# A message-passing layer on one Trainium2 core: v's products among the tiles of the sums, a head in halves, and a reordered end

## The chip, the cores and the metric

The program runs on one core of a Trainium2 chip. The metric is the device time of one execution in microseconds (us), as a median of several executions. Engines are called by their short names: PE does the matrix products (PEld is its loading of weights), DVE and ACT do elementwise work, POOL issues the indirect DMAs here, and SP issues the other DMAs.

## The reference

A graph has N = 12500 nodes with 128 features, and 412500 edges with 20 features and a weight each. The edges come sorted by `dst`; their `src` is in no order.

```python
h = jnp.maximum(_layernorm(x, axis=-1), 0.0)
# inside the layer: idx_i = src, idx_j = dst, f_ij = edge_attr_20, rcut_ij = edge_weight
def ssp(x):
    return jax.nn.softplus(x) - LOG2
h = x @ W_in2f                                   # x is the h above
Wij = ssp(f_ij @ W_f1 + b_f1) @ W_f2 + b_f2
Wij = Wij * rcut_ij[:, None]
x_ij = h[idx_j] * Wij
agg = jax.ops.segment_sum(x_ij, idx_i, num_segments=h.shape[0])
out = ssp(agg @ W_o1 + b_o1) @ W_o2 + b_o2
...
    x = x + _L0_gnn_ref(h, ...)
    return x
```

So each edge gets a filter vector (two small layers with a softplus between), which is multiplied with the row of h of its dst; the products, called messages here, are summed by src, and a two-layer output is added to x.

## The kernel before, in words

**Tiles and stages.** The edges are worked through in 806 chunks of 512, four chunks to a group. A chunk has QT = 4 tiles of 128 edges. `step(k)` (L993) is called once for each chunk k, and for a while after the last one; it holds one link of a software pipeline, so that it touches chunks k to k+6 and more. The instruction order on every engine is the order in which the code issues them (a manual schedule, the loop at L1216). A queue runs its instructions in that order, and an instruction that waits holds up all behind it on its engine.

The way of a chunk c through the pipeline:

- *hidden* (PE, L691): the edge features times W_f1, for a pair of chunks at once, into the PSUM tile z of 2 x 512 columns.
- *log* (ACT, L700, L701, L703): absolute value, exponential and logarithm, which make the softplus, again 2 x 512 wide. `softplus_logs` (L403 to L405) is the exponential and the logarithm alone; the finish uses it 512 wide behind its own absolute value (L439).
- *end* (DVE, L709): max(z, -b) plus that logarithm gives r.
- *bias* (ACT, L793): a PSUM bank of tag "v" is filled with a bias row; *value* (PE, L801) adds r @ W_f2 to it in four products. This is v, the filter of the chunk.
- *window* (DVE, L785) and *pick* (PE, L812): a one-hot matrix picks the rows of h of the dst nodes out of a window of rows ("near") that SP loads; *picked* (ACT, L822) multiplies them with the edge weight and gives hg.
- *blocks*, *rank* (DVE L714, PE L733 and L766, DVE L738): for each edge, the place of its message in a table of slots.
- *message* (DVE, L830): o = v * hg, and POOL issues four indirect DMAs (L834) that scatter the 512 rows to their slots.

The tag "v" has three PSUM banks, which v and the picked rows share.

**Segments and sums.** The 202 groups are cut in 7 segments of 88, 44, 30, 14, 14, 8 and 4 groups. Each segment has its own table of slots, with room for each block of 128 nodes. Seven steps (DELAY) after the last chunk of a segment, its table is read back while later chunks go on: a Collect loads units of up to 6 tiles (SP, L873), *compare* (DVE, L886) makes one-hot matrices `to`, *add* (PE, L907) sums tile after tile into a PSUM bank that holds four blocks of nodes ("acc"), and *keep* moves a finished bank to `agg` (ACT, L928, for the first segment; an add on DVE, L930, for the others). Which units are summed in which step is planned ahead (L1070 to L1102): a rate in tiles a step follows from the work left and from `end = NCH + BEYOND`, and at most one bank ends in a step. The units of a step are compared in it; the adds come one unit later, so that one unit is always left over.

So there are steps without sums (before the first segment is done) and steps with sums, some steps with sums alone after the last chunk, and then a last part in which the last segment is summed and the output layers (*finish*, L428) run, quad by quad of 512 nodes.

**The order in a step.** In step k the code issues: the loads; the message of k and its scatters; what is left of the ranks (DVE); keep for the banks that the step before finished (DVE or ACT); picked(k+1) on ACT and value(k+1) on PE; pick(k+2) on PE and bias(k+2) on ACT; window (DVE); end (DVE); blocks (DVE); the compares (DVE); rank (PE); log (ACT); hidden (PE); the adds of the sums (PE). On PE alone this is value, pick, rank, hidden, sums, and then the next step's value. A first product of value, pick and hidden also waits for a scatter of eight chunks earlier (BACK = 8, `behind`).

**Head.** Before the loop the first quads of h are made: `make_h` (L326 to L393) normalises 512 rows of x, multiplies them with W_in2f and splits the result (PSUM, hps) in three bf16 parts: hb's first is a copy (L367), the rest goes to a tile `left` in SBUF (DVE, L370), its bf16 copy is the second (L371), and the rest of that the third (DVE, L373). The bias of the features' layer and its product with W_f2 are made in `biases` (L302, its matmul L307, DVE's L308). The parts are stored, and the window's rows are loaded from there. The loop starts at k = -3.

**x for the end.** The output is added to x. From step XK = 300 on quads of x are loaded ahead (`x_ahead`, NX = 14 of 25 quads early), and the bias b_o2 is added to them (`x_bias`, on DVE for the early ones, on POOL for those after the last chunk) from a row spread over all partitions in SBUF (bo2).

## Time and profile before

| | us |
|---|---|
| median of ten executions | 5290.81 |
| the ten, lowest to highest | 5267.05 to 5316.33 |
| the profiled execution, its own time | 5285.38 |
| its span | 5283.6 |

| engine | busy us | share of the span | instructions |
|---|---|---|---|
| PE | 3706.6 | 70% | 21594 |
| PEld | 2833.7 | 54% | |
| DVE | 3140.5 | 59% | 7101 |
| ACT | 2788.9 | 53% | 5466 |
| POOL | 3145.4 | 60% | 3292 |

The clock that PE was granted was 0.764 of full speed on the mean. The DMA engines moved 820.65 MB, 155 GB/s.

A busy time is the time in which an engine had an instruction in work; what an engine spends on issuing a DMA or on waiting is not in it. In the rows of the trace, a mark such as [0.49 <-DVE to L886] says that the engine had been idle for 0.49 us before the instruction and what released it; x22 counts the instructions that the row puts together; `out<-in` gives the tiles that an instruction writes and reads. A PE product shows as two records (f32). A stretch is given from the span's start in us. The profiled execution is one of the program as it runs, so a sum of durations from it is made against its own time, and not against the median.

### The profile page before, as it was taken

What the parts mean: (1) busy time and instruction counts of PE and PEld (TensorE: products, weight loads), DVE (VectorE), ACT (ScalarE), POOL (GpSimd) and SP (SyncE); (2) the same over time, 40 slices, a digit from 0 to 9 for tenths busy, and PEclk for the clock granted to TensorE, in tenths of its full rate; (3) what the DMA queues carried; (4) which work ended last, traced back from release to release, by engine and by line L of the source; (5) the groups of instructions that cost most, each with busy time, mean ns of one, the idle gap of its engine ahead of it and who ended that gap; (6) DMA issues with size and microseconds to landing.
All of it is one profiled execution on the core that took longest, in us unless ns stands there. A gap on an engine that the chain in (4) does not pass through costs nothing. (4 is left out here: it accounts for less than half of the span.)

```text
span 5283.6 us, 74340 instructions
## 1 busy us (share of the span) xinstructions
PE 3706.6 (70%) x21594; PEld 2833.7 (54%) x21594; DVE 3140.5 (59%) x7101; ACT 2788.9 (53%) x5466; POOL 3145.4 (60%) x3292
## 2 busy tenths in 40 slices
PE   5565555555655555688888788787777777777778
PEld 3343334443433333466666666666666656666667
DVE  5555555555444454566666666566666666666667
ACT  5555555555555555555555555455554544555443
POOL 5666666666666666666665665555655555655552
PEclk8666666666666666688888888888887888888889
DMA  4545444444433344465656555556555655665546
GB/s 141 155 142 155 140 145 143 126 147 126 117 99 93 100 120 131 124 184 176 182 178 206 172 168 173 159 174 199 177 164 162 200 170 153 176 190 157 163 131 195
DMA packets 515221, 820.65 MB, mean 155 GB/s; under 512 B 177188, under 2 KB 312728, under 8 KB 514812
## 3 DMA queue, kind: packets, MB, share of 16 engines
q1 hardware_dynamic: 411212, 602.55, 39.7%
q0 software_dynamic: 103168, 213.15, 12.1%
q8 instruction: 180, 2.95, 0.2%
q14 instruction: 229, 1.88, 0.1%
q10 hardware_dynamic: 432, 0.13, 0.0%
HBM read 419.75 MB, written 395.69 MB: 154 GB/s over the span
## 5 line engine op out<-in xcount | busy, mean ns | idle before, releaser
L834 POOL DMA_INDIRECT slots<-o,slot x3224 | 3107.6, 964 | 2042.3 <-DVE o L830 1154.4
L822 ACT ACTIVATE hg<-picked,rcut 128x128 f32<-128x128 f32 x3224 | 915.2, 366 | 1390.3 <-remote 696.6
L907 PEld LDWEIGHTS acc<-to,m 128*128 128x128 f32 x8152 | 1203.4, 230 | 458.3 <-issue 324.2
L907 PE MATMUL acc<-to,m 128*128 128x128 f32 x8152 | 1302.2, 320 | 177.2 <-issue 108.5
L801 PEld LDWEIGHTS v<-wf,r 128*128 128x128 f32 x6448 | 1067.3, 245 | 397.0 <-issue 278.6
L801 PE MATMUL v<-wf,r 128*128 128x128 f32 x6448 | 1161.9, 334 | 133.2 <-issue 88.8
L830 DVE TENSOR_TENSOR o<-v,hg 128x512 f32<-128x512 f32 x806 | 552.3, 685 | 974.6 <-remote 498.9
L691 PE MATMUL z<-f,wf 20*128 20x512 f32 x1612 | 632.0, 861 | 481.0 <-DVE r L709 293.0
L886 DVE TENSOR_TENSOR to<-count_ps,m 128x640 f32<-128x640 f32 (+3 forms) x793 | 636.9, 826 | 279.8 <-remote 104.3
L793 ACT ACTIVATE v<-bf 128x512 f32<-128x512 f32 x806 | 486.0, 603 | 453.6 <-DVE o L830 273.6
L738 DVE TENSOR_REDUCE top<-free 128x4 f32<-128x392 f32 x806 | 448.2, 556 | 441.6 <-remote 289.6
L812 PE MATMUL picked<-near,at 96*128 96x128 bf16 x3224 | 386.7, 253 | 421.9 <-DVE o L830 301.4
L709 DVE SCALAR_TENSOR_TENSOR r<-z,nbf,a 128x1024 f32<-128x1024 f32 x403 | 513.9, 1275 | 94.2 <-issue 51.4
L812 PEld LDWEIGHTS <-at 96*128 96x128 bf16 x3224 | 307.0, 116 | 478.9 <-issue 453.1
L766 PE MATMUL free<-inb,rest_of 128*128 128x392 f16 x806 | 326.3, 405 | 333.7 <-issue 205.5
L700 ACT ACTIVATE a<-z,bf 128x1024 f32<-128x1024 f32 x403 | 445.2, 1105 | 195.5 <-remote 69.7
L691 PEld LDWEIGHTS z<-f,wf 20*128 20x128 f32 x1612 | 157.8, 235 | 691.4 <-DVE r L709 390.7
L703 ACT ACTIVATE a<-a,half 128x1024 f32<-128x1024 f32 x403 | 462.7, 1148 | 13.1
L714 DVE TENSOR_TENSOR inb<-count_ps,blk 128x392 f16<-128x392 f32 x806 | 445.4, 553 | 0.0
L701 ACT ACTIVATE a<-a 128x1024 f32<-128x1024 f32 x403 | 425.9, 1057 | 12.8
L733 PE MATMUL free<-inb,after 128*128 128x392 f16 x806 | 329.4, 409 | 7.9 <-issue 3.9
L785 DVE TENSOR_SCALAR at<-rel,prow 96x512 bf16<-96x512 bf16 x806 | 284.4, 353 | 0.0
(113 smaller groups left out, 1230.4 us busy)
## 6 DMA issues: line engine op xcount, KB each, us to landing
m<-slots SPq DMA_DIRECT2D x307, 387.0 KB
m<-slots SPq DMA_DIRECT2D x278, 322.5 KB
rel<-rel_d SPq DMA_DIRECT2D x202, 384.0 KB
slots<-o,slot POOLq DMA_INDIRECT x3224
m<-slots SPq DMA_DIRECT2D x193, 258.0 KB
slots<-zero SPq DMA_DIRECT2D x96, 387.0 KB
f<-in_f_t SPq DMA_DIRECT2D x404, 80.0 KB
slots<-zero SPq DMA_DIRECT2D x58, 516.0 KB
```

The costliest lines, as they stand in the source:

```text
L691: mm = nc.tensor.matmul(z[:, k, :], wf1[rows, :], self.f[rows, :], start=True, stop=True)
L703: nc.scalar.activation(a, a, AF.Ln, bias=half, scale=0.5)
L709: nc.vector.scalar_tensor_tensor(r, z, nbf1, a, op0=ALU.max, op1=ALU.add)
L738: nc.vector.tensor_reduce(self.top[:, c * QT:(c + 1) * QT], free_v, axis=mybir.AxisListType.X, op=ALU.max)
L793: nc.scalar.activation(v, spread(bf12, QT), AF.Copy)
L801: mm = nc.tensor.matmul(v[:, i, :], r[:, i * P:(i + 1) * P], wf2, start=False, stop=True, skip_group_check=True)
L812: mm = nc.tensor.matmul(ps[:, i, :], at[:, i * P:(i + 1) * P], near, start=i == 0, stop=i == QT - 1, skip_group_check=True)
L822: nc.scalar.activation(hg[:, i, :], ps[:, i, :], AF.Copy, scale=self.rcut[:, j:j + 1])
L830: nc.vector.tensor_mul(o[:, :, :P], v, hg)
L834: put = nc.gpsimd.indirect_dma_start(out=views[j % VIEWS], out_offset=bass.IndirectOffsetOnAxis(ap=self.slot[:, j:j + 1], axis=0), in_=o[: ...
L886: nc.vector.tensor_tensor(to[:, :n, :], count_ps[:, None, :].to_broadcast([P, n, P]), m[:, :n, P:].to_broadcast([P, n, P]), op=ALU.is_equal)
L907: nc.tensor.matmul(self.acc[b // QT][:, i, :], m[:, j, :P], to[:, j, :], start=t == 0, stop=t == self.seg.tiles(b) - 1)
```

## The change

Six things are changed in one.

1. *v among the sums.* In a step with sums, value(k+2) is issued at the end of step k, one product after every second tile of the sums; what is left of its four products follows the last tile. It is value(k+1) at the start of step k+1 that is left out for it. For this `value` and `add` become generators (`values`, `adding`). In steps without sums nothing moves.
2. *Head in halves.* The logarithm and the end of the first pair of chunks are done in halves of 512 (`half_log`, `half_end`), value(0) is issued before the loop, in steps 0, 2 and 4 (HEAD) the log comes earlier and the end later, the message of chunk k+1 is issued within step k for k = 0 to 3, and the second quad of h goes on after message 0.
3. *Order at the end.* BEYOND goes from 14 to 8. In steps after the last chunk that have units, keep comes after the first compare and no longer before it.
4. *make_h.* The tile `left` falls away: the rest is formed in place in PSUM (hps).
5. *b_o2 from PSUM.* It is copied once to PSUM (bo2_ps, in the bank of count_ps), and the early quads of x take it from there.
6. *More early quads.* NX goes from 14 to 16, and the tag xo has 8 buffers in place of 6.

```diff
@@ -366,11 +366,10 @@
         hb = ln.tile([P, QT, 3, P], BF16, name="hb")
         nc.scalar.activation(hb[:, :n, 0, :], hps[:, :n, :], AF.Copy)
         yield
-        left = ln.tile([P, QT, P], F32, name="left")
-        nc.vector.tensor_sub(left[:, :n, :], hps[:, :n, :], hb[:, :n, 0, :])
-        nc.scalar.activation(hb[:, :n, 1, :], left[:, :n, :], AF.Copy)
+        nc.vector.tensor_sub(hps[:, :n, :], hps[:, :n, :], hb[:, :n, 0, :])
+        nc.scalar.activation(hb[:, :n, 1, :], hps[:, :n, :], AF.Copy)
         yield
-        nc.vector.tensor_sub(hb[:, :n, 2, :], left[:, :n, :], hb[:, :n, 1, :])
+        nc.vector.tensor_sub(hb[:, :n, 2, :], hps[:, :n, :], hb[:, :n, 1, :])
         for (b, rows), table in zip(tables, h3_t):
             lo = max(0, b - q * QN) // P
             hi = min(n, (b + rows - q * QN) // P)
@@ -420,10 +419,10 @@
         for p, cs, rows in pieces:
             nc.sync.dma_start(xo[:p, cs, :], x[rows, :].rearrange("(c p) f -> p c f", p=p))
 
-    def x_bias(xo, pieces, engine=nc.vector):
+    def x_bias(xo, pieces, engine=nc.vector, b=bo2):
         for p, cs, rows in pieces:
             xi = xo[:p, cs, :]
-            engine.tensor_add(xi, xi, spread(bo2[:p, :], xi.shape[1]))
+            engine.tensor_add(xi, xi, spread(b[:p, :], xi.shape[1]))
 
     def finish(t0, n, sT, quad, psum, z, xo=None, bank=("v", 3)):
 
@@ -547,7 +546,8 @@
         free_v = free.rearrange("p (t b) -> p t b", b=NBLK)
 
 
-        count_ps = state_ps.tile([P, P], F32, name="count_ps")
+        numbers = state_ps.tile([P, CH], F32, name="numbers")
+        count_ps, bo2_ps = numbers[:, :P], numbers[:, P:2 * P]
 
         def clear(seg):
 
@@ -702,6 +702,20 @@
                 self.pair[c] = z, a
                 nc.scalar.activation(a, a, AF.Ln, bias=half, scale=0.5)
 
+            def half_log(self, k):
+                if k == 0:
+                    self.half = self.pair[0], quad.tile([P, 2, CH], F32, name="a", bufs=2)
+                z, a = (t[:, k, :] for t in self.half)
+                nc.scalar.activation(a, z, AF.Abs, bias=bf1)
+                softplus_logs(a)
+
+            def half_end(self, k):
+                if k == 0:
+                    self.pair[0] = quad.tile([P, 2, CH], F32, name="r")
+                z, a = (t[:, k, :] for t in self.half)
+                nc.vector.scalar_tensor_tensor(self.pair[0][:, k, :], z, nbf1, a,
+                                               op0=ALU.max, op1=ALU.add)
+
             def hidden_end(self, c):
 
                 z, a = self.pair[c]
@@ -793,7 +807,7 @@
                 nc.scalar.activation(v, spread(bf12, QT), AF.Copy)
                 return v
 
-            def value(self, c, v):
+            def values(self, c, v):
 
                 r = self.pair[c // 2 * 2][:, c % 2, :]
                 k = self.g * NCHUNK + c - 1
@@ -802,6 +816,12 @@
                                           start=False, stop=True, skip_group_check=True)
                     if i == 0:
                         behind(mm, k, k % 2)
+                    yield
+
+            def value(self, c, v):
+
+                for _ in self.values(c, v):
+                    pass
                 return v
 
             def pick(self, c, at, ps):
@@ -894,6 +914,11 @@
                 self.to[u] = to
 
             def add(self, u):
+                for _ in self.adding(u):
+                    pass
+
+            def adding(self, u):
+
                 b0, nb, t0, nt = self.units[u]
                 m, to = self.m.pop(u), self.to.pop(u)
                 for j in range(nb * nt):
@@ -909,6 +934,7 @@
                     if t == self.seg.tiles(b) - 1 and (i == QT - 1 or b == NBLK - 1):
                         self.done.append(b)
                         owed.append(self)
+                    yield
 
             def ends(self, u):
 
@@ -934,7 +960,8 @@
         groups = {}
         NEXT = table_of.index(1) - 1
         LG, LW, LR, LZ = 12, 6, 6, 4
-        DELAY, BEYOND = 7, 14
+        DELAY, BEYOND = 7, 8
+        HEAD = (0, 2, 4)
 
         def of(k):
             return groups[k // NCHUNK], k % NCHUNK
@@ -1009,29 +1036,42 @@
 
             if k in vs:
                 message(k)
+            if not k:
+                next(h[1])
             for r in tops:
                 for _ in r:
                     pass
             tops.clear()
-            for c in owed:
-                c.keep()
-            owed.clear()
+            def keep():
+                for c in owed:
+                    c.keep()
+                owed.clear()
+
+            if k < NCH or not units:
+                keep()
             if has(k + 1):
                 g, c = of(k + 1)
                 hgs[k + 1] = g.picked(c, ps.pop(k + 1))
-                vs[k + 1] = g.value(c, bs.pop(k + 1))
+                if k + 1 not in vs:
+                    vs[k + 1] = g.value(c, bs.pop(k + 1))
+            if k in HEAD:
+                part("log", k + LZ - 1, pairs(hidden_log))
             if has(k + 2):
                 g, c = of(k + 2)
-                ps[k + 2] = psum.tile([P, QT, P], F32, name="picked", tag="v", bufs=3)
+                if k + 2 not in ps:
+                    ps[k + 2] = psum.tile([P, QT, P], F32, name="picked", tag="v", bufs=3)
                 g.pick(c, ats.pop(k + 2), ps[k + 2])
                 if k + 2 > 0:
                     bs[k + 2] = g.bias(c)
             part("window", k + 3, window)
-            if k:
+            if k not in HEAD:
                 part("end", min(k + LZ - 2, made.get("log", -1)), pairs(hidden_end))
             part("blocks", min(k + LR + 1, 2 * k + 3), blocks)
             for c, u in units:
                 c.compare(u)
+                keep()
+            if 0 <= k < HEAD[-1]:
+                message(k + 1)
             upto = max(made["rank"], min(k + LR, 2 * k + 3))
             ready = [ranks(j) for j in range(made["rank"] + 1, upto + 1)]
             made["rank"] = upto
@@ -1041,15 +1081,27 @@
             for r in ready[-1:]:
                 next(r, None)
                 tops.append(r)
-            part("log", min(k + LZ - 1, made["hidden"]), pairs(hidden_log))
-            if not k:
-                message(1)
+            if k in HEAD:
                 part("end", made["log"] - 1, pairs(hidden_end))
-            part("hidden", k + LZ if k > -2 else 1, pairs(hidden))
+            elif k != -1:
+                part("log", min(k + LZ - 1, made["hidden"]), pairs(hidden_log))
+            if k not in HEAD[:-1]:
+                part("hidden", k + LZ, pairs(hidden))
+            between = iter(())
+            if units and k + 2 in bs and k + 2 <= made["end"] // 2 * 2 + 1:
+                g, c = of(k + 2)
+                vs[k + 2] = bs.pop(k + 2)
+                between = g.values(c, vs[k + 2])
+            n = 0
             for c, u in units:
                 if summed:
-                    summed[0].add(summed[1])
+                    for _ in summed[0].adding(summed[1]):
+                        n += 1
+                        if n % 2 == 0:
+                            next(between, None)
                 summed[:] = c, u
+            for _ in between:
+                pass
 
         zeros = {}
         units = {}
@@ -1101,7 +1153,7 @@
                 if todo[i - 1][1].ends(todo[i - 1][2]):
                     break
 
-        def x_ahead(homes, engine):
+        def x_ahead(homes, engine, b):
 
             pending = []
             for q, xo in homes:
@@ -1113,23 +1165,23 @@
                 yield
                 yield
                 if len(pending) > 2:
-                    x_bias(*pending.pop(0), engine)
+                    x_bias(*pending.pop(0), engine, b)
             for w in pending:
                 yield
-                x_bias(*w, engine)
+                x_bias(*w, engine, b)
 
         def as_quad(t):
             return t.rearrange("p (c f) -> p c f", f=P)
 
         xs = {}
-        NX = 14
+        NX = 16
 
         def early_homes():
             for q in range(NX):
-                if q < 6:
-                    yield q, quad.tile([P, QT, P], F32, name="xo", bufs=6)
-                elif q < 12:
-                    yield q, ln.tile([P, QT, P], F32, name="xo", tag=("xb", "xT", "left")[q // 2 - 3],
+                if q < 8:
+                    yield q, quad.tile([P, QT, P], F32, name="xo", bufs=8)
+                elif q < 14:
+                    yield q, ln.tile([P, QT, P], F32, name="xo", tag=("xb", "xT", "left")[q // 2 - 4],
                                      bufs=2)
                 else:
                     t = ln.tile([P, QT, 3, P], BF16, name="xo", tag="hb", bufs=2)
@@ -1166,6 +1218,7 @@
                     yield
             yield from ranges(psum)
             late_biases(psum)
+            nc.scalar.activation(bo2_ps, bo2, AF.Copy)
 
         def side():
 
@@ -1197,22 +1250,27 @@
             groups[0].blocks(0)
             made["blocks"] = 0
             next(h[0])
-            part("log", 0, hidden_log)
+            groups[0].half_log(0)
             next(h[0])
             part("rows", 3, rows)
             biases(psum)
             bs[0] = groups[0].bias(0)
+            groups[0].half_log(1)
+            made["log"] = 0
             ready = ranks(0)
             next(ready)
             groups[0].starts()
-            part("end", 0, hidden_end)
+            groups[0].half_end(0)
             part("window", 0, window)
+            vs[0] = groups[0].value(0, bs.pop(0))
             next(ready, None)
             made["rank"] = 0
+            groups[0].half_end(1)
+            made["end"] = 0
             group(1)
             aside = side()
-            x_early = x_ahead(early_homes(), nc.vector)
-            x_late = x_ahead(late_homes(), nc.gpsimd)
+            x_early = x_ahead(early_homes(), nc.vector, bo2_ps)
+            x_late = x_ahead(late_homes(), nc.gpsimd, bo2)
             for k in range(-3, max(NCH, max(units) + 1)):
                 for seg, d in zeros.get(k, ()):
                     seg.clears.append(nc.sync.dma_start(*d).ins.name)
@@ -1225,7 +1283,7 @@
                     kept["rest"] = True
                 step(k, now)
 
-                if k >= -1:
+                if k >= 0:
                     for m in h:
                         next(m, None)
                 if k > NEXT - 3:
```

## The prediction

> **What bounds the kernel now.** I read the time by stages first, then who waited for whom, then a stretch of the timeline. The table of stretches (PE, PEld, DVE, ACT, POOL busy, granted clock, DMA share, GB/s):
>
> ```profile
> 0.00:62.00 62.00, 37.41 (x179) 25.11 (x180) 45.96 (x152) 37.71 (x73) 27.11 (x44) 0.92 0.48 141
> 62.00:2230.00 2168.00, 1254.04 (x5908) 848.62 (x5907) 1120.49 (x2888) 1211.27 (x2399) 1365.11 (x1412) 0.65 0.44 130
> 2230.00:5147.00 2917.00, 2300.19 (x14717) 1862.66 (x14715) 1876.83 (x3908) 1489.69 (x2920) 1713.19 (x1783) 0.83 0.58 173
> 5147.00:5202.00 55.00, 44.23 (x334) 40.22 (x333) 38.39 (x61) 0.00 (x0) 18.89 (x18) 0.95 0.89 258
> 5202.00:5283.60 81.60, 70.76 (x462) 57.09 (x462) 58.78 (x95) 50.24 (x75) 21.11 (x36) 0.99 0.55 153
> ```
>
> These are the head, the 352 steps without sums, the 446 steps with sums, the steps after the last chunk, and the finish. A step costs 6.16 us without sums (2168/352) and 6.54 us with them (2917/446). No engine is full in either. Four scatters of a chunk take POOL 4 x (0.96 + 0.30 issue) = 5.05 us, so POOL would be the floor; what lies above it is POOL waiting. The waits of the steps with sums:
>
> ```profile
> POOL slots L834 <- DVE o L830: 724.6, 264, 10.1
> ...
> DVE o L830 <- remote: 192.3, 54, 6.0
> ...
> DVE o L830 <- PE acc L907: 134.4, 38, 5.1
> ...
> DVE agg L930 <- remote: 96.1, 19, 7.9
> ```
>
> POOL waits for the message's multiply (L830), which itself waits, as does DVE's add into the sums (L930). "remote" is a release whose source the profile does not tell. By the view of line L830 the message waited 466 us in 153 waits in this stage. One such wait in the timeline:
>
> ```profile
> 2454.70 4.79 PE L907 MATMUL acc<-to,m 128*128 128x128 f32 x22
> ...
> 2459.32 1.06 PE L801 MATMUL v<-wf,r 128*128 128x128 f32 x8
> 2459.58 0.95 POOL L834 DMA_INDIRECT slots<-o,slot  x1 [0.30 <-issue]
> ...
> 2460.77 1.50 PE L907 MATMUL acc<-to,m 128*128 128x128 f32 x12
> ...
> 2461.97 0.69 DVE L830 TENSOR_TENSOR o<-v,hg 128x512 f32<-128x512 f32 x1 [3.83 <-PE free L733]
> ...
> 2462.93 0.95 POOL L834 DMA_INDIRECT slots<-o,slot  x1 [2.40 <-DVE o L830]
> ```
>
> The reader is to see two things. v's products (x8, two records for each product) stand behind 11 tiles of sums (x22), so this message cannot start before 2460.4. And it starts 1.6 us after that still, at 2461.97, when POOL has run dry. POOL's pattern is a burst of two or three chunks, then a gap; two chunks and a gap of 2.4 us give the 12.5 us that I find again and again here.
>
> **The change part by part.** The sum is made against the profiled execution (5285.4 us; span 5283.6). The median of the ten runs shown is 5290.8, so 5.4 us are added at the end.
>
> *v among the sums.* On PE the products of chunk k+2 stood right behind the sums of step k, as the first work of step k+1. They move forward only by the sums that come after them: one product stands after every second tile, so the fourth stands after the eighth. Counting L907's matmuls between two groups of L801 in the trace, 247 of 444 steps have more than 8 tiles, 755 tiles beyond the eighth in all; in the others v ends where it did. A tile is two records: 4.79/22 x 2 = 0.435 us in the stretch above, at half clock, and 1.50/12 x 2 = 0.25 us at full. A granted clock of 0.83 between half and full is 34% of the time at half, so 0.31 us a tile: 755 x 0.31 = 236 us, or 0.96 us in each of the 247 steps. Of the waits before messages, 100 follow such a step: 100 x 0.96 = 96 us if all of it reaches POOL. Against that: only 19 of the waits (20 us) end within 0.25 us of v's end; in the rest the release comes later, as at 2461.97. So the bounds are 0 and -96; I take the middle, **-48**. No new wait stands in front of the sums: the bias copy (L793) that v is added to ended a median of 3.5 us before the step's third tile, and was later than it in 8 steps, 6 us in all. r (L709) must be there before the hidden matmul (L691), which stands ahead of the sums already. No instruction is added.
>
> *The sums end later.* What v gains, the last tiles lose: up to four products, 1.06 us (x8 at full clock) to 1.92 (the same x8 at half, seen at 1500.31), 1.35 us at this stage's clock. Behind the last tile stand DVE's L930 (66 waits, 204 us here) and the compares L886 (149 waits, 279 us; 72 of them put down to L907), and behind these, on DVE, the window, r, the blocks and the next message. Lower bound: 0, as the message later in the same step waits anyway and takes the delay up (466 us of such waits). Upper bound: 66 x 1.35 = 89 us, and 72 x 0.68 = 49 for the compares. I take **+22**, a quarter of the L930 part, since a bank ends in only 104 of the 446 steps on DVE and most messages have slack there.
>
> *The head.* POOL starts at 23.24 us and then stands before chunks 1, 2 and 4 for 2.13, 2.49 and 3.82 us; without the usual 0.30 that is 7.5 us, the most to be had. First the added work: two half logarithms cost 2 x (0.687 + 0.630 + 0.722) = 4.08 us of ACT (rows of L439, L404, L405, 512 wide) in place of 3.31 (L700, L701, L703), and two half ends 1.5 in place of 1.28. The first message does not come earlier by it: its pick (L812) waited for the near rows until 19.64. What comes earlier is v of chunk 0 (2.0 us of PE at 20.01, now before the pick), the second pair's z, which stood at 23.05 in front of v of chunk 1 (25.05), and DVE's work on the second quad, now behind the message. The first quad's PSUM bank is held until L373 ends (14.34) and not L370 (12.95), so the bias matmul L307 slips from 13.53 to about 14.4 and DVE's L308 with it; DVE had 0.30 idle before L709 to hide it, the rest is about 0.6 us. Bounds +2 and -7.5; I take **-4**, about half of the idle.
>
> *The end.* BEYOND goes from 14 to 8, which raises the last rate from 9.81 tiles a step to 13.73. Worked through, the plan of units comes out the same step by step, since a step stops at the first bank that ends: **0**. What acts is the order of DVE. Here is a step after the last chunk:
>
> ```profile
> 5158.07 0.69 DVE L930 TENSOR_TENSOR agg<-agg,acc 128x512 f32<-128x512 f32 x1 [0.65 <-PE acc L907]
> ...
> 5158.67 1.28 DVE L886 TENSOR_TENSOR to<-count_ps,m 128x512 f32<-128x512 f32 x2
> ...
> 5159.41 2.05 PE L907 MATMUL acc<-to,m 128*128 128x128 f32 x16 [0.49 <-DVE to L886]
> 5160.61 0.69 DVE L930 TENSOR_TENSOR agg<-agg,acc 128x512 f32<-128x512 f32 x1 [0.65 <-PE acc L907]
> ```
>
> The period is 2.54 us: PE waits 0.49 for the first compare, which waits for L930, which waits for PE. With the compare ahead of L930 that ring is open, and PE's 2.05 us would be left: 15 such steps x 0.49 = 7.4 us. But something is late next: DMA. From 5156 to 5202 the windows give 20 us at 257, 18 at 277 and 8 at 279 GB/s, 12.4 MB, with the share at 0.98 in the last. Less two x quads (0.5 MB), which now load some 490 steps earlier, that is 11.8 MB; at 279/0.98 = 285 GB/s it takes 41.5 us for 46. Bounds 0 and -7.4; I take **-4**. The finish after 5202 is not touched: PE is busy there 70.8 of 81.6 us.
>
> *Operands from PSUM.* L370 (one operand in PSUM) takes 686 ns and L373 (both in SBUF) 679: with 25 of L373's kind and 16 bias adds now reading PSUM, 41 x 7 ns = 0.3 us of DVE, spread over steps in which DVE idles over 2 us. The copy of bo2 is one ACT instruction of 0.3 us. Its cover is that idle time; without it 0.6 us. **0**. A rule speaks against this edit: the Trainium skill, "Perfetto Trace Analysis", § Optimizing Scalar/DVE Operations, puts the overhead of a DVE instruction at about 60 ns on SBUF and 125 on PSUM. By that the 41 would cost 2.7 us, a tenth of which the rows show, and the total would be 3 us worse if nothing hid it.
>
> **Sum:** -48 + 22 - 4 - 4 = -34. 5285.4 - 34 = 5251; on the scale of the runs shown 5290.8 - 34 = **5257 us**.
>
> **Rivals.** *The message is held by something other than v.* For it: 129 of 148 measured waits, 441 us, do not end with v's last product, and in the stretch above message and scatter go on only after POOL has emptied its burst. Then v's place and the sums' later end both fall into time in which everything stands, and head and end alone are left: 5290.8 - 8 = 5283, no change. Against it: the messages that wait longest, 2.2 us on the mean, follow steps with 12 tiles, and those after 5 tiles wait 0.5.
>
> *The sums' end decides (slower).* Place: L930 in the steps with sums, ahead of all other DVE work of its step; price: 1.35 us at each of its 66 waits, 89 us, when the message's waits do not take them up. With v's gain at 20 (the true waits) and head and end as above: 89 - 20 - 8 = +61, so 5352 us. It decides from the point where the later end costs more than v gains with head and end, 56 us of 138 possible. For it: PE granted 0.83 and DVE (64% busy) are both well filled here, and L930 stands in front. Against it: PE does the same work in the same total order, and what follows the sums on PE (the pick) starts when it did.
>
> **How the numbers follow.** A measurement of this kernel tells 0.3%, 16 us, from no change. Forecast (v's gain counts, 5257, own range 5205 to 5274) 0.45; held elsewhere (5283) 0.19; sums' end decides (5352) 0.36. That gives faster 0.46, same 0.18, slower 0.36. The low end takes most of v's bound with head and end, 5290.8 - 80 - 12 = 5199, say 5195; the high end is the slow rival's 5352.
>
> **What would show it.** Right: the steps with sums fall from 2917 us to about 2890, the wait before L830 there from 466 to below 420, and L930's wait grows from 204 by 20 or so; chunk 7's first scatter, at 67.08 now, comes near 63; the period of 2.54 us after the last chunk becomes 2.1 to 2.4. Wrong: L930's and L886's waits grow by more than L830's fall; POOL's two-chunk period stays at 12.5 us; or PE's granted clock in the stage moves off 0.83, which would change every term by more than the order does.

## The result and the profile after

The changed kernel takes 5405.72 us (median of 13 runs, 5389.79 to 5421.39), the one before 5293.81 us (46 runs): a ratio of 1.021, with 1.0194 to 1.0226 as its 95% interval. The forecast was 34 us faster; it is 112 us slower. The profiled execution has a span of 5411.6 us. The sets of runs below came to different chips, so ratios are always taken to the kernel before in the same set.

The table of stretches of the changed kernel, with the same columns as before (PE, PEld, DVE, ACT, POOL busy, granted clock, DMA share, GB/s); head, steps without sums, steps with sums, steps after the last chunk, finish:

```profile
0.00:62.00 62.00, 37.48 (x162) 24.15 (x163) 42.80 (x144) 35.05 (x68) 25.98 (x44) 0.94 0.47 137
62.00:2244.00 2182.00, 1262.32 (x5917) 861.85 (x5916) 1124.40 (x2896) 1213.17 (x2408) 1356.11 (x1410) 0.65 0.44 129
2244.00:5283.00 3039.00, 2342.52 (x14718) 1894.68 (x14719) 1882.31 (x3911) 1492.42 (x2920) 1717.02 (x1788) 0.82 0.55 166
5283.00:5330.00 47.00, 42.15 (x339) 39.50 (x338) 38.65 (x61) 0.00 (x0) 14.63 (x14) 0.99 0.96 290
5330.00:5411.60 81.60, 70.76 (x462) 57.09 (x462) 58.74 (x95) 50.24 (x75) 21.11 (x36) 0.97 0.55 152
```

The loss is in the third row: 3039 us where it was 2917. DVE, ACT and POOL are busy for as long as before (1882, 1492, 1717 us), PE for 42 us more, at 0.82 of its clock in place of 0.83. So work did not grow by the loss; idle time did. The second row is 14 us longer too, though v does not move there. Message 359, the first of the steps with sums, comes at 2230.82 us before and 2244.78 after, but also at 2228.25 in b_to4 and 2241.5 in c_v_after_rank, which change no order ahead of it; so these 14 us are within what chips and executions differ by. The waits in that stretch (engine and line, what released it, us in total, times, longest); L850 is the message, L752 the rank's reduce, L906 the compares and L956 keep, which were L830, L738, L886 and L930:

```profile
POOL slots L854 <- DVE o L850: 833.3, 254, 10.2
...
DVE to L906 <- remote: 219.0, 60, 7.2
...
DVE to L906 <- PE acc L932: 120.8, 67, 5.8
...
DVE agg L956 <- remote: 103.7, 22, 7.5
DVE agg L956 <- PE acc L932: 99.1, 35, 5.4
...
DVE top L752 <- remote: 94.7, 22, 7.7
...
DVE o L850 <- remote: 72.0, 34, 5.4
```

Of the compares' rows, the two largest were in the kernel before:

```profile
DVE to L886 <- remote: 104.3, 32, 5.1
DVE to L886 <- PE acc L907: 100.0, 72, 5.0
```

POOL waits for the message for 833 us in place of 725, although the message itself waits far less: its largest row is 72 us where it was 192. Summing in the traces the idle time right ahead of each line, from chunk 359 to the last:

| DVE idle ahead of | before, us | after, us |
|---|---|---|
| message | 463 | 195 |
| rank's reduce | 52 | 189 |
| compares | 280 | 453 |
| keep | 204 | 272 |
| all four | 999 | 1109 |

The message gained 268 us and the three others lost 378, 110 net; the stretch between the same two messages grew from 2915 to 3037 us, 122. One such case, in the timeline of the changed kernel:

```profile
2510.76 0.33 PE L747 MATMUL free<-inb,after 128*128 128x392 f16 x1
...
2512.28 0.69 DVE L850 TENSOR_TENSOR o<-v,hg 128x512 f32<-128x512 f32 x1 [1.39 <-PE free L747]
...
2517.91 0.57 DVE L752 TENSOR_REDUCE top<-free 128x4 f32<-128x392 f32 x1 [4.94 <-remote]
2518.04 0.96 POOL L854 DMA_INDIRECT slots<-o,slot  x1 [0.30 <-issue]
2518.39 0.34 DVE L799 TENSOR_SCALAR at<-rel,prow 96x512 bf16<-96x512 bf16 x1
...
2518.65 1.27 DVE L723 SCALAR_TENSOR_TENSOR r<-z,nbf,a 128x1024 f32<-128x1024 f32 x1
...
2519.85 0.55 DVE L728 TENSOR_TENSOR inb<-numbers,blk 128x392 f16<-128x392 f32 x1
...
2520.32 1.81 DVE L906 TENSOR_TENSOR to<-numbers,m 128x768 f32<-128x768 f32 x2
...
2522.05 0.16 DVE L849 COPY o<-place 128x4 f32<-128x4 f32 x1
...
2522.52 0.69 DVE L850 TENSOR_TENSOR o<-v,hg 128x512 f32<-128x512 f32 x1 [0.31 <-ACT hg L842]
...
2523.49 0.96 POOL L854 DMA_INDIRECT slots<-o,slot  x1 [4.49 <-DVE o L850]
```

The message goes at 2512.28 and starts a burst of scatters. DVE's next instruction, the reduce, reads a rank whose product ended at 2511.09 by the trace, yet it starts at 2517.91, when the burst is nearly over. Then all of DVE's work of the step (window, r, blocks, two compares) still stands ahead of the next message, and POOL, dry since 2519.00, waits 4.49 us. Had the message been the instruction that waited, only its own 0.85 us of DVE's work (L849 and L850) would have stood there, by these rows.

**A table of POOL's gaps.** For every gap of POOL over 1 us in that stretch I took the last DVE instruction with more than 0.5 us of idle time ahead of it, that is, the wait that was open last. In the changed kernel such a gap lasts 2.46 us on the mean where that was the message, 3.49 at a compare, 4.01 at keep, 4.30 at the reduce. Times are ratios to the kernel before in the same set (95% interval). The gaps are those of one profiled execution of each kernel, and the row of the kernel before is its trace of the first set; the ratios are of all executions:

| kernel | ends at message / compare / keep / reduce | gaps, us | ratio |
|---|---|---|---|
| before | 136 / 61 / 39 / 2 | 714 | 1 |
| after | 67 / 96 / 55 / 21 | 835 | 1.021 (1.0194 to 1.0226) |
| a_v_back | 146 / 51 / 41 / 0 | 721 | 1.0013 (0.9995 to 1.0031) |
| b_v_only | 84 / 88 / 53 / 11 | 811 | 1.0185 (1.0143 to 1.0227) |
| b_v_late | 90 / 86 / 56 / 5 | 788 | 1.0158 (1.0119 to 1.0197) |
| b_v_first | 10 / 118 / 58 / 37 | 928 | 1.0359 (1.0315 to 1.0402) |
| a_top_first | 3 / 60 / 28 / 133 | 895 | 1.0342 (1.0306 to 1.0377) |
| b_to4 | 177 / 11 / 48 / 1 | 686 | 0.9941 (0.9921 to 0.9961) |
| b_v_to4 | 114 / 24 / 65 / 29 | 785 | 1.0106 (1.0069 to 1.0143) |
| b_hidden_last | 143 / 38 / 39 / 2 | 718 | 0.9974 (0.9954 to 0.9993) |
| c_v_after_rank | 206 / 42 / 13 / 0 | 772 | 1.0083 (1.0058 to 1.0108) |
| c_to4_keep | 176 / 12 / 34 / 6 | 641 | 0.9853 (0.9828 to 0.9878) |
| d_v_keep | 131 / 22 / 51 / 32 | 765 | 0.9982 (0.996 to 1.0004) |
| d_v_keep_top | 151 / 26 / 48 / 2 | 768 | 0.9925 (0.9894 to 0.9956) |
| d_keep_top | 185 / 20 / 32 / 0 | 706 | 0.9896 (0.9846 to 0.9946) |

### The profile page after: what moved, and what is told of

Read it like the earlier page. It is cut to its first block, busy times and chain, and to the rows that moved or that the text cites. A ratio compares the mean times of both kernels' runs of the same rounds, so it can differ in the third digit from the quotient of the medians.

```text
span 5411.6 us, 74225 instructions
## 1 busy us (share of the span) xinstructions
PE 3755.2 (69%) x21594; PEld 2877.3 (53%) x21594; DVE 3146.9 (58%) x7104; ACT 2790.9 (52%) x5470; POOL 3134.9 (58%) x3290
## 3 DMA queue, kind: packets, MB, share of 16 engines
q8 instruction: 180, 2.95, 0.2%
## 5 line engine op out<-in xcount | busy, mean ns | idle before, releaser
L932 PE MATMUL acc<-to,m 128*128 128x128 f32 x8152 | 1524.5, 318 | 199.7 <-issue 125.9
L932 PEld LDWEIGHTS acc<-to,m 128*128 128x128 f32 x8152 | 1314.4, 227 | 493.3 <-issue 350.2
L815 PE MATMUL v<-wf,r 128*128 128x128 f32 x6448 | 1410.8, 347 | 121.7 <-ACT v L807 62.2
L815 PEld LDWEIGHTS v<-wf,r 128*128 128x128 f32 x6448 | 1223.7, 257 | 366.7 <-issue 235.0
L850 DVE TENSOR_TENSOR o<-v,hg 128x512 f32<-128x512 f32 x806 | 551.9, 685 | 692.1 <-remote 354.9
L906 DVE TENSOR_TENSOR to<-numbers,m 128x640 f32<-128x640 f32 (+3 forms) x793 | 641.1, 827 | 458.5 <-remote 219.0
L752 DVE TENSOR_REDUCE top<-free 128x4 f32<-128x392 f32 x806 | 448.6, 557 | 594.9 <-remote 418.8
L728 DVE TENSOR_TENSOR inb<-numbers,blk 128x392 f16<-128x392 f32 x806 | 445.3, 553 | 0.0
L747 PEld LDWEIGHTS <-after 128*128 128x128 f16 x806 | 91.3, 113 | 409.5 <-issue 404.9
```

What stands on the lines that cost most here:

```text
L752: nc.vector.tensor_reduce(self.top[:, c * QT:(c + 1) * QT], free_v, axis=mybir.AxisListType.X, op=ALU.max)
L815: mm = nc.tensor.matmul(v[:, i, :], r[:, i * P:(i + 1) * P], wf2, start=False, stop=True, skip_group_check=True)
L850: nc.vector.tensor_mul(o[:, :, :P], v, hg)
L906: nc.vector.tensor_tensor(to[:, :n, :], count_ps[:, None, :].to_broadcast([P, n, P]), m[:, :n, P:].to_broadcast([P, n, P]), op=ALU.is_equal)
L932: nc.tensor.matmul(self.acc[b // QT][:, i, :], m[:, j, :P], to[:, j, :], start=t == 0, stop=t == self.seg.tiles(b) - 1)
```

## The experiments

**Which part costs it.** *a_v_back* is the changed kernel with the interleaving undone:

```diff
-            between = iter(())
-            if units and k + 2 in bs and k + 2 <= made["end"] // 2 * 2 + 1:
...
             for c, u in units:
                 if summed:
-                    for _ in summed[0].adding(summed[1]):
...
+                    summed[0].add(summed[1])
                 summed[:] = c, u
```

> The changed kernel with one part undone: v's four products stand at the start of the next step again, behind the sums; head, end and PSUM operands stay changed. If the products among the sums cost the whole loss, this is at 5280 to 5297 us (ratio to before 0.998 to 1.001), with the steps after the last chunk some 8 us shorter and the head some 4 to 10 us longer than before. If the head or the end costs part of it, it stays above 5310 us.

*b_v_only* is the kernel before with nothing but that interleaving:

```diff
+            between = iter(())
+            if units and k + 2 in bs and k + 2 <= made["end"] // 2 * 2 + 1:
...
+                        if n % 2 == 0:
+                            next(between, None)
```

> The kernel before with nothing but v's products one by one after every second tile. If they cost the whole loss: 5395 to 5420 us (ratio 1.019 to 1.024). If the parts act on each other, it stays below 5370 us.

a_v_back takes 5299.69 us against 5296.9 before, and b_v_only 5391.23, a little under its range of 5395 to 5420: the interleaving makes the loss, within the intervals the whole of it. Head, end and PSUM operands together are worth nothing that shows.

**Where v stands.** *b_v_first* puts all four products ahead of the sums, *b_v_late* among the last eight tiles; both start from the kernel before, and are shown against b_v_only:

```diff
 # b_v_first
+            for _ in between:
+                pass
             for c, u in units:
...
 # b_v_late
+            n = -sum(c.units[u][1] * c.units[u][3]
+                     for c, u in ([tuple(summed)] if summed else []) + list(units[:-1]))
...
-                        if n % 2 == 0:
+                        if n in (-7, -5, -3, -1):
```

> The kernel before with all four products of v ahead of the step's sums, in one block. Theory S (the sums end later, and what stands behind the last tile on DVE is late): the sums end four products later in every step with units, so at least as slow as the changed kernel, 5400 to 5450 us. Theory H (the message comes earlier, POOL starts a burst earlier, and the rank's reduce and the compares wait instead for releases that come late while POOL scatters): v comes earlier still, 5400 to 5500 us, with the message's wait under 200 us and that of the reduce over 180 us. Theory X (PE itself pays for going to and fro between two sorts of products): no going to and fro is left, below 5330 us.

> The kernel before with v's products one by one among the last eight tiles, the fourth ahead of the last tile, so that v ends one tile earlier than before, at most, in steps of more than eight tiles, while the sums end up to four products later, as in the changed kernel. Theory S: as slow as the changed kernel, 5390 to 5420 us. Theory H: v is hardly earlier in the 247 long steps, which leaves half the loss or less, below 5350 us. Theory X: the same going to and fro, 5390 to 5420 us.

X falls: with no going to and fro the loss is almost twice as large. Between S and H the pair is undecided: first, at 5489 us, lies above S's range and inside H's, and late, at 5375 us, between the two. b_v_first shows where the waits go when the message has almost none. Its message waits 15 us in all, and these are its largest DVE waits:

```profile
DVE to L892 <- remote: 250.6, 60, 8.4
DVE top L738 <- remote: 220.3, 31, 10.9
DVE to L892 <- PE acc L918: 157.4, 71, 6.0
```

What the message no longer waits, compares and reduce do, and POOL's gaps grow to 928 us.

**Buffers, and the reduce ahead of the message.** *b_to4* and *b_v_to4* give the compares' tile a fourth buffer, *a_top_first* moves the loop over `tops` ahead of `message(k)` in the changed kernel, *b_hidden_last* moves the hidden products behind the sums:

```diff
 # b_to4, b_v_to4
-                to = edge.tile([P, UT, P], F32, name="to", bufs=3)
+                to = edge.tile([P, UT, P], F32, name="to", bufs=4)
 # a_top_first
+            for r in tops:
+                for _ in r:
+                    pass
+            tops.clear()
             if k in vs:
                 message(k)
             if not k:
                 next(h[1])
-            for r in tops:
...
 # b_hidden_last
-            part("hidden", k + LZ if k > -2 else 1, pairs(hidden))
+            if not units:
+                part("hidden", k + LZ if k > -2 else 1, pairs(hidden))
             for c, u in units:
...
+            if units:
+                part("hidden", k + LZ, pairs(hidden))
```

> The kernel before with four buffers for the compares' tile (to) in place of three. If a compare waits for the sums of two units earlier to give its buffer back (theory S by way of the buffers), the compares' wait in the steps with sums falls from 280 us to 150 or less, and the time by 0.3 to 1.5%: 5215 to 5280 us. If the compares wait for something else (the tables' loads, or releases that come late while POOL scatters, theory H), no change: 5285 to 5310 us.

> The kernel before with v's products among the sums and four buffers for the compares' tile. Theory S by way of the buffers: the compares' wait falls from 428 us (with three) to below 280, and the time from ratio 1.0185 to 1.010 or less. Theory H, or S by way of the banks (keep) alone: the wait stays above 350 us and the ratio at 1.015 to 1.022.

> The changed kernel with the rank's reduce (top) ahead of the message on DVE, so that its release can't be held up by the scatters that this message starts. Theory H: the reduce's wait falls from 189 us to 100 or less, the compares' with it, and the time to 5330 to 5370 us. Theory S: what is late are the sums, and the message now starts 0.55 us later in each step besides: 5400 to 5480 us.

> The kernel before with the hidden products (a pair of 512 wide matmuls in every second step) behind the step's sums in place of ahead of them: the sums end some 1.7 us earlier in these steps, and v starts where it did, as the order of sums and hidden products is the only thing that moves. Theory S: the opposite sign of the change, 0.3 to 1% faster, 5240 to 5280 us, with less wait before the compares (280 us before) and before L930 (204 us). If the sums' end decides nothing by itself: 5285 to 5320 us.

The buffer takes the compares' idle time from 280 to 47 us, and the time to 5273.25 from 5302.07. But the message then waits 655 us in place of 463; its rows in b_to4:

```profile
DVE o L830 <- remote: 289.5, 77, 6.9
DVE o L830 <- PE acc L907: 163.2, 44, 5.4
DVE agg L930 <- remote: 103.1, 21, 7.0
```

So 233 us less of one wait and 192 more of the other are worth 29 us. That the compares wait for a buffer which the sums two units earlier give back, as S had it by way of the buffers, is thereby shown: H forecast no change. With v among the sums the same holds of the wait (428 us in b_v_only, 91 in b_v_to4), and the ratio of 1.0106 lies just above S's bound of 1.010 and below H's range. But what is left of the loss, 1.0106 / 0.9941 = 1.017, is nearly what it was: the compares are not the whole cause.

a_top_first went against H: 5490.62 us, which is also a little above S's 5400 to 5480. H had the reduce's release held up by the scatters of this very message; in fact 126 of its 134 waits over 1 us end while POOL is dry. That changed the theory. **R**: what PE finishes while POOL scatters reaches DVE late, mostly some 1.6 us after POOL has run dry (the median over the gaps that end at a message or a compare is 1.57 to 1.64 us, before and after). A gap of POOL is the time until that release and whatever DVE has to do from that instruction to the message: on the mean 1.1 and 1.4 us at a message, 1.3 and 2.2 at a compare in the kernel before. At keep and at the reduce R does not hold as it stands. There, in the changed kernel, the release comes 0.1 us (keep) and 1.3 us (reduce) before POOL runs dry in the median, but on the mean 4.6 and 5.5 us then pass until POOL goes on, where it is 1.7 at a message. With the reduce in front of the message, 1.9 us pass from its release on. b_hidden_last, where the sums end earlier, gains 0.26%, at the edge of what can be told: S by the end of the sums alone is weak.

**The opposite move.** *b_v_after_rank* issues `value(k + 1)` behind the hidden products of step k, *b_v_last* behind the sums of step k; *b_to4_v_after_rank* adds the buffer, and *b_to4_end* is b_to4 with the changed kernel's BEYOND and its keep after the first compare.

```diff
 # b_v_after_rank; in b_v_last the lower lines stand behind the loop over the units
-                vs[k + 1] = g.value(c, bs.pop(k + 1))
+                if not units:
+                    vs[k + 1] = g.value(c, bs.pop(k + 1))
...
             part("hidden", k + LZ if k > -2 else 1, pairs(hidden))
+            if units and has(k + 1):
+                g, c = of(k + 1)
+                vs[k + 1] = g.value(c, bs.pop(k + 1))
```

> The opposite move: the kernel before, but in steps with units v's products of chunk k+1 stand later on PE, behind the pick, the rank and the hidden products of step k and ahead of that step's sums, so that v is 1.3 to 3 us later and the sums end when they did. Theory R, formed from the traces so far (what PE makes while POOL scatters reaches DVE 1.6 us after POOL runs dry, all at once; the gap of POOL is then 1.6 us and the work that DVE does from the wait that stood open to the next message; so the best wait is the one right before the message): more gaps that end at the message (136 of 245 in the trace before, here over 170), fewer that end at a compare (61) or at L930 (39), and 0.2 to 1% faster, 5245 to 5290 us. If v's lateness is what counts (my prediction's first term): slower by 50 to 150 us, 5350 to 5450. Theory S (the end of the sums): no change, 5285 to 5315 us.

> The same move taken to its end: v of chunk k+1 behind the sums of step k itself, so that the message of the next step waits for compares and sums of the step before it. Theory R alone: every gap ends at the message, faster still, 5180 to 5260 us. But the ring from one message over the compares, the sums and v to the next message then has one step in place of two, some 7 us by my sum; if that decides, slower: over 5450 us. Theory S: the sums end earlier by v's 1.35 us, faster, 5200 to 5280 us.

> v behind the rank and hidden products as in the run before the last, and four buffers for the compares' tile. Theory R: both take gaps away from compares, so the two gains (0.6% with the buffers alone) add up in part only: 5240 to 5275 us, with hardly a gap that ends at a compare. If v's lateness counts: 5330 us or more.

> The kernel before with four buffers for the compares' tile and the changed kernel's end alone (BEYOND 8, keep behind the first compare in the steps after the last chunk; 14 early quads as before). The buffers alone gave 0.994 of the time before (5273 us). If the end is worth what I put down (4 us, at most 7.4): 5262 to 5273 us, and a period of the steps after the last chunk of 2.1 to 2.4 us in place of 2.54; if the transfers take the gain back: 5270 to 5280 us.

This set came to a chip on which the kernel before takes 4226.3 us, so that none of the absolute times applies. The ratios: 1.0269 (1.0255 to 1.0283), 1.216 (1.2142 to 1.2179), 1.0258 (1.0231 to 1.0284) and 0.9988 (0.9979 to 0.9997). There a chunk takes 5.08 us in the steps without sums, which is POOL's own time, and b_to4_end has no gap of POOL over 1 us in the steps with sums. In its waits POOL's largest row is the plain issue, and the message's 72 us:

```profile
POOL slots L834 <- issue: 429.7, 1409, 0.3
...
DVE o L830 <- PE v L801: 71.7, 49, 3.3
```

On this chip a later v costs time (1.0269), as my first term has it with the sign turned, and the fourth buffer takes next to nothing of that (1.0258). b_v_last shows what a ring of one step costs: 1.216, with 7.16 us a step in the steps with sums where some 7 were expected, and all of its 255 gaps end at the message.

**Again, on other chips.** *c_after* is the changed kernel, *c_v_after_rank* the run above once more, and *c_to4_keep* is b_to4_end with keep moved:

```diff
-            if k < NCH or not units:
+            if not units:
                 keep()
...
             part("blocks", min(k + LR + 1, 2 * k + 3), blocks)
+            if k < NCH:
+                keep()
             for c, u in units:
                 c.compare(u)
                 keep()
```

> The changed kernel itself, beside the one before on the same chip. On a chip where PE's releases come late while POOL scatters (the kernel before at about 5290 us): 1.018 to 1.024 of the time before, as on the first chip. On a chip where they come at once (the kernel before at about 4226 us, POOL's 5.05 us a chunk as the floor): theory R leaves nothing of the loss, as no wait holds a release back: 0.995 to 1.005. Theory S (the sums end later on PE, whatever POOL does): still slower, 1.01 to 1.025, also there.

> The kernel before with v of chunk k+1 behind the rank and hidden products of step k, again, as the run of it before fell on a chip on which PE's releases come at once (1.027 of the time before there: v's lateness counts). On such a chip: 1.02 to 1.03 again. On a chip where the releases come late, theory R: more gaps of POOL that end at the message (136 of 245 in the kernel before), 0.99 to 1.00 of the time before; if v's lateness outweighs that: 1.01 to 1.04.

> The kernel before with four buffers for the compares' tile, the changed kernel's end alone, and keep (L930 on DVE) behind window, end and blocks in place of ahead of them in the steps with units: DVE does 1 to 2 us of work that waits for nothing before it waits for the sums. On a chip with late releases, theory R: the 48 gaps that end at keep (170 us with the four buffers) shrink by 1 to 1.5 us each, 50 to 70 us, of which some is lost since the bank comes free later: 0.980 to 0.992 of the time before. If keep's wait is not what holds POOL: 0.993 to 0.997. On a chip with releases at once: 0.996 to 1.001.

The kernel before took 5294.27 us here. c_after repeats the loss (1.0184, 1.0156 to 1.0212). c_v_after_rank does what R says of the gaps, 206 end at the message, but not of the time: 1.0083. A gap at the message is 2.95 us on the mean there, not 2.45: from release to restart it is shorter (1.13 us, before 1.38), but the release comes 1.8 us after POOL ran dry (2.95 less 1.13) where it came after 1.1. No burst of three chunks is left either (six before). The ratio lies between the two forecasts, R's 0.99 to 1.00 and the 1.01 to 1.04 of a later v that outweighs it. R's sign failed: the order of the waits is what it says, but a later v costs more than that order gives. c_to4_keep is the best kernel of the study, 5219.99 us, 0.9853. POOL's gaps fall by another 45 us (686 to 641), and keep's largest row is now

```profile
DVE agg L930 <- remote: 76.5, 19, 6.0
```

where b_to4 has 103.1 in it. The work did not change; only window, end and blocks now stand ahead of the wait and no longer behind it. Some 8 us of the gain belong to the changed end (138.7 us from the last message on in b_to4, 130.6 here). And R had the gaps at keep shorter by 1 to 1.5 us each: they are fewer, 34 in place of 48, and on the mean hardly shorter (3.4 us, before 3.5).

**Taking the loss apart.** *d_v_keep* is c_to4_keep with v among the sums, *d_v_keep_top* also has the loop over `tops` behind the blocks, *d_keep_top* is that without v among the sums.

```diff
-            for r in tops:
-                for _ in r:
-                    pass
-            tops.clear()
...
+            if not units:
+                finish_tops()
...
             part("blocks", min(k + LR + 1, 2 * k + 3), blocks)
+            finish_tops()
             if k < NCH:
                 keep()
```

> The best kernel so far (four buffers for the compares' tile, keep behind window, end and blocks, the changed kernel's end: 0.9853 of the time before) with v's products among the sums again. Chip with late releases, theory R: the compares' share of the loss is gone with the buffers, the part of the reduce (top, 30 gaps of some 4 us) stays: 0.993 to 1.003. Theory S: the same delay of the sums, the same loss of 1.8 to 2% as without the buffers: 1.003 to 1.006. Chip with releases at once (before at about 4226 us): R 0.995 to 1.003, S 1.01 to 1.025.

> The same with the rank's reduce (top) too behind window, end and blocks, so that DVE has its free work done before the first wait that an early message leaves open. Late releases, theory R: most of what is left of the loss goes, 0.985 to 0.995, with under 15 gaps of POOL that end at top. Theory S: as the run before it, or slower by what the later reduce holds up the rank on PE. Releases at once: within 0.5% of the run before it.

> The best kernel so far with the reduce moved as in the run before, without v among the sums. The reduce hardly waits there (55 us in all with four buffers), so that little is to be had: 0.980 to 0.990 by R with late releases; slower, 0.99 to 1.00, if the later reduce holds up the rank on PE more than it frees.

The kernel before took 5387.77 us in this set. With the reduce moved, only 2 gaps end at it in place of 32, and the interleaving costs 0.9925 / 0.9896 = 1.003, within the intervals; it was 1.0185 alone and 1.017 with the buffer, and with keep moved too it is 0.9982 / 0.9853 = 1.013, across two sets. All three kernels lie inside R's ranges, and S, by which the sums' later end costs 1.8 to 2% in each, does not hold for the last pair. The traces show this less clearly than the medians. POOL's gaps are 768 us in d_v_keep_top, no less than the 765 in d_v_keep, as more of them now end at the message; in d_keep_top they are 706. And the profiled executions of the last pair lie further apart (5382.6 and 5327.5 us, 1.0%) than the medians (5353.11 and 5337.35), so a rest of up to about 1% for the later sums is not excluded.

## Why the prediction was wrong

- *What bounds the kernel.* Right as far as it went: POOL would be the floor, and what lies above it is POOL's waiting. I had even noted that this message went on only when POOL had run dry, and gave it to a rival of no change.
- *v among the sums, -48.* This is the step that failed. The message's idle time fell by 268 us, more than my bound of 96, and it was worth less than nothing: with nothing else changed, b_v_only takes 1.0185 of the time before. (The bound itself counts 755 tiles beyond the eighth; with the last steps left out, as the text means it, the trace has 688, which would make 87 of the 96.) I priced a wait ahead of the message by what disappears there, and took it that POOL would start earlier and stay so. The runs showed in its place that an early message only opens the next wait, at the reduce, a compare or keep (378 us more before the three), that this wait lasts until about the end of the burst, and that more of DVE's step stands behind it: 2.2 to 5.5 us from release to POOL's next scatter, on the mean, where it is 1.7 at the message. The sentence that no new wait stands in front of the sums was nearly true (v's products waited 22 us for the bias copy, 3 before) and beside the point: the new waits stand behind the message.
- *The sums end later, +22 (0 to 138).* The place was right, the size too small: keep +67 us, compares +173. The reduce, +137, was not in it at all, as I followed only what waits for the sums and not what follows the message on DVE. My slow rival (5352 us) had the right side, and L930 as its mechanism; L930 is the smallest of the three, and the rival's time lay 54 us below the result. The compares' share goes with the fourth buffer (428 us of idle time in b_v_only, 91 in b_v_to4); the sum has the compares in its upper bound alone, with 49 us. Nor would the sign that I named for being wrong, L930's and L886's waits growing by more than L830's fall, have shown it: they grew by 240 us, less than 268; only with the reduce does the balance turn.
- *Held elsewhere (5283).* Its premise held, and its conclusion, that v's place then does not matter, did not.
- *The head, -4.* No gain: chunk 12's message stands at 95.46 us before, 98.91 in the changed kernel, 95.51 in c_after and 94.88 in a_v_back. Chunk 7's first scatter is at 67.79, not near 63: POOL idles less before chunks 1 and 4 (0.30 and 1.99 us), but now 2.14 us before chunk 3 and 3.85 before chunk 5, at 57.68.
- *The end, -4 (0 to -7.4).* Right in kind, and in all but one trace nearer the upper bound than the middle: from the last message to the end it is 138.0 us before, 129.8 after, 132.1 in c_after, 130.6 in c_to4_keep, but 136.2 in a_v_back, which has the same end. Keep follows keep after 2.2 us on the mean, as forecast, where it was 2.54. DMA takes over as said, at 290 GB/s and a share of 0.96.
- *BEYOND and the PSUM operands, 0.* Nothing shows: the first subtraction takes 682 ns on the mean where it was 676, the early bias adds 673 where they were 677, and a_v_back is at the time of before.

## What to carry to other kernels

A wait that is taken away is worth what the next wait on that engine leaves of it: list all that the engine waits for in a step and ask, for each, what work stands between it and the instruction that feeds the bounding queue. Put work that waits for nothing ahead of the waits of an in-order engine; here that, with a fourth buffer and the changed end (c_to4_keep, 0.985), gave the best time, while no kernel with an earlier v was faster than the same one without. Give a buffer that is only waited for by accident one more copy before moving products about.

## What the runs showed of the hardware

The traces also record when a semaphore changes. From the end of a PE product that signals to the next change of PE's semaphore it takes, in the steps with sums of the changed kernel, 1.3 us in the median and over 5.1 us in a tenth of the cases while POOL has a scatter in work or stands in the 0.3 us between two, and 0.01 and 1.0 us while it has none; in the kernel before 1.2 and 4.85, against 0.01 and 0.9. On the chip of 4226 us it is 0.01 us in the median and at most 0.02 in nine of ten cases, with a scatter in work (b_to4_end). PE is not alone in this: in the changed kernel ACT's and DVE's changes come 1.1 and 0.5 us after the end in the median with a scatter in work, and 0.01 us without; in b_to4_end they come after 0.01 us with one. The Trainium skill, "Perfetto Trace Analysis", § Tensor Engine Instruction (MATMUL, LD_WEIGHTS), says that the end of a PE instruction in a profile is estimated from its size and not observed, while the semaphore is pushed when PSUM has acknowledged the bytes; that allows for such a lag, but the chip without it ran the same instructions under the same estimate. Some changes are missing from the records (3006 changes for 3666 products), so the lags are rather too long; in b_to4_end nearly all are there (3713 of 3747). Why the releases come late in the other sets and not in that one was not tried, and stays open; so does what the change itself does where they come at once. The kernel before takes 20% less time on that chip (4226.3 against 5294.27 us), some ten times what the change moved. How much of this is the lag was not taken apart: the granted clock differs as well, 0.83 against 0.76.
